# A graph network on one core: relational tables as two fp32r parts instead of three bf16 parts, and the loads at the start of the second relational layer issued earlier

## The chip, the cores and the metric

The kernel runs on one core of a Trainium2 chip. The metric is the device time of one execution in microseconds (us), lower is better. The median of three runs before the change is 2020.77 us (2017.62 to 2021.79). The outputs must equal the reference's to float32 accuracy, up to a tolerance.

## The reference

A graph has 3125 nodes of 128 features and 100,000 edges (`src`, `dst`, sorted by `dst`), each with one of 8 types. Four graph networks run one after the other, each added to its input and normalised. The first three (three graph convolutions, one sum over neighbours, one isomorphism layer with two batch norms) are dense products with an adjacency matrix that the kernel builds. The change is in the fourth, a relational network of two layers:

```python
def rgcn_layer(x, src, dst, etype, W, W_root, b, num_rels):
    N = x.shape[0]
    do = W.shape[-1]
    h = jnp.einsum('ni,rio->rno', x, W)
    msg = h[etype, src]
    seg = dst * num_rels + etype
    sums = jax.ops.segment_sum(msg, seg, num_segments=N * num_rels)
    cnt = jax.ops.segment_sum(jnp.ones(msg.shape[0], x.dtype), seg, num_segments=N * num_rels)
    mean = sums / jnp.maximum(cnt, 1.0)[:, None]
    agg = mean.reshape(N, num_rels, do).sum(axis=1)
    return agg + x @ W_root + b
src, dst = (edge_index[0], edge_index[1])
h = rgcn_layer(x, src, dst, edge_type, W1, root1, b1, NUM_RELS)
h = jax.nn.relu(h)
return rgcn_layer(h, src, dst, edge_type, W2, root2, b2, NUM_RELS)
```

For every node and every edge type, the rows of the sources are averaged; the averages go through (layer one) or come out of (layer two) a matrix for each type.

## The kernel before

**Blocks and two ways of summing.** The nodes are 25 blocks of 128. For the first 15 blocks of destinations (`ND`, in the chunks `DENSE` of 4, 4, 4 and 3 blocks) the sum over edges of a type is a dense product: matrices of edge counts, bytes in DRAM (`rel`), are loaded by `load8` (L755) on SP's DMA queue, five source blocks at a time, cast to fp32r by `cast8` (L763) on ScalarE or VectorE, and multiplied by the table of source rows in `relation` (L873, matmul at L885). The table stands in SBUF as two fp32r parts, a rounded value and its rest (`split2`, L786; tile `hilo`), so each of 25 source blocks takes two matmuls of 512 (or 384) columns. For the last 10 blocks (`NG`) edges are **gathered**, 128 at a time, in tiles: `gathered` (L893) runs over 10 groups of up to 34 tiles, 321 in a layer. For a tile an indirect DMA on GpSimd's queue (L919) fetches 128 rows of the table from DRAM into `gx`; VectorE makes a one-hot matrix `oh` for four tiles at a time (L909) of 24 destinations x 8 types = 192 columns; TensorE multiplies each part of the rows by it (L927) into two PSUM banks of 512 columns. A tile whose 192 columns cross column 512 is split into two matmuls a part.

**Tables in DRAM.** For the gathering, x3 (the input of layer one) is stored in `xt_d`, and x after the first layer's matrices, one row for each type and node, in `ht_d`. Both hold a row as three bf16 parts that add up to the float32 value. `store3` (L792) makes them: ScalarE rounds, VectorE subtracts, ScalarE rounds the rest, VectorE subtracts again, and SP's queue stores the 768 bytes a row.

**Order.** The order is written out by hand: `gathered` is a generator, and after every five source blocks of a dense product (ten matmuls) `fill` (L866) runs it some steps on, about 1.9 in layer one and 2.1 in layer two; a step is a tile. In layer one, each finished chunk goes through `linear1` (L950), which multiplies by the matrices of both layers and stores `ht_d` with `store3` (L978); gathered chunks do so too, from `put1`. After the last dense chunk the rest of the gathering runs alone (L1014).

**Between the layers.** In layer two `fetch(r)` (L1018) brings `ht_d`'s rows for type r back in five pieces: a load on SP's queue into `back`, two additions on VectorE that rebuild float32 (L1027, L1028), and `split2` into a `hilo` pair (L789 on ScalarE, L790 on VectorE). `fetch(0)` is called at L1068, when layer one has ended; `fetch(r + 1)` after the first chunk of type r. The final products with `root2` (L1036) go ahead of the first dense product. In layer two all five casts of a chunk are ScalarE's (L1073); in layer one, VectorE takes three of five.

**Making x3.** In a loop over seven chunks (L849), TensorE transposes, `normalise` runs on VectorE and ScalarE, `split2` fills the pair `xs`, and `stored` (L846) calls `store3` for `xt_d`. Tiles of a pool have a fixed number of buffers (`bufs`); a tile's writer waits until the readers of the buffer's earlier content are done. `hilo` and `hT` share two buffers with the tag "big".

## Time and profile before

The profiled execution took 2027.4 us, its span from the first to the last instruction is 2025.5 us; the three timed runs lie between 2017.62 and 2021.79. Mean granted TensorE clock 0.975.

| engine | busy us | share of span | instructions |
|---|---|---|---|
| TensorE (PE) matmul | 1794.3 | 89% | 11523 |
| TensorE weight load (PEld) | 1387.0 | 68% | 11523 |
| VectorE (DVE) | 1205.1 | 59% | 2055 |
| ScalarE (ACT) | 1253.0 | 62% | 1118 |
| GpSimd (POOL) | 859.5 | 42% | 717 |

Stages, by the first and last start of their lines: lists and matrices until 408 us; the dense networks (L628) 408 to 835; x3 from 835; layer one's dense products from 861, its gathers 895 to 1485, its end near 1511; layer two from 1511 to the end.

The costliest groups of the relational part (engine, line, operation, shape, count, busy us, mean ns of one):

| group | count | busy us | mean ns |
|---|---|---|---|
| PE L885 fp32r matmul, 512 columns | 2400 | 622.2 | 405 |
| PE L885 fp32r matmul, 384 columns | 800 | 170.1 | 357 |
| PEld L885 weight load 128x128 f32 | 3200 | 576.5 | 190 |
| PE L927 bf16 matmul, 192 columns | 1644 | 194.1 | 250 |
| PE L927 bf16 matmul, 160 / 32 columns | 114 / 114 | 16.3 / 14.2 | 233 / 178 |
| PE L927 bf16 matmul, 128 / 64 columns | 114 / 114 | 15.5 / 14.3 | 221 / 193 |
| PE L927 bf16 matmul, 96 columns | 108 | 8.0 | 206 |
| PEld L927 weight load 128x128 bf16 | 2208 | 157.0 | 97 |
| ACT L767 cast to fp32r, 2560 / 1920 | 169 / 56 | 388.3 / 99.3 | 2329 / 1794 |
| DVE L767 cast to fp32r, 2560 / 1920 | 71 / 24 | 125.4 / 33.0 | 1769 / 1376 |
| POOL L919 gather from xt_d | 321 | 366.1 | 1140 |
| POOL L919 gather from ht_d | 321 | 326.2 | 1016 |
| DVE L909 one-hot, 768 bf16 | 152 | 83.9 | 553 |
| DVE L1027, L1028, L790 (640 each) | 40 each | 32.6, 32.4, 32.1 | 824, 824, 822 |
| ACT L789 (640) | 40 | 27.8 | 723 |
| store3 of ht_d: ACT L798, L800; DVE L799, L801 | 50 to 54 each | 29.2, 33.4; 34.3, 37.2 | 583, 619; 686, 689 |

Matmuls are pipelined, and the mean of one contains its latency; the cost of one in a row of them is the distance from start to start. "PE" is the multiplication, "PEld" the load of its stationary operand, which overlaps it. A releaser is what ended an idle time; "issue" means that the profile shows nothing that the engine waited for.

### The profile page before, as it was taken

To read this page: it belongs to the slowest core of one execution; us is meant where nothing else is said; L and a number is where in the kernel's file an instruction comes from. 1 tells how busy PE (TensorE), PEld (TensorE's weight loads), DVE (VectorE), ACT (ScalarE), POOL (GpSimd) and SP (SyncE) were. 2 spreads that over 40 slices of the span, in tenths; PEclk is the share of its full clock that TensorE was granted. 3 is DMA by queue.
4 is the path that set the end of the run, shared out by engine and by line. 5 is a ranking of instruction groups with operands and counts; after the bars stand their busy time and mean duration, and the time that the engine had idled before them with its cause. 6 is when DMAs were issued, how large, how long until landed. Compare 5 with 4: busy or idle time off the path is not lost.

```text
span 2025.5 us, 30183 instructions
## 1 busy us (share of the span) xinstructions
PE 1794.3 (89%) x11523; PEld 1387.0 (68%) x11523; DVE 1205.1 (59%) x2055; ACT 1253.0 (62%) x1118; POOL 859.5 (42%) x717
## 2 busy tenths in 40 slices
PE   2677676669999999889999999999999999999897
PEld 1555555458888888667577567758757777777676
DVE  6999998777768863475455345435346444434424
ACT  3999997757888666663233333233338777777774
POOL 5315624120000000027777267706716666666664
PEclk9999998889999999999999999999999999999998
DMA  4766776667888887477677457737659887888773
GB/s 100 277 271 266 291 287 237 247 189 232 255 259 257 251 268 235 140 225 190 177 212 207 148 171 209 188 101 198 184 151 269 243 228 220 235 240 245 196 204 101
DMA packets 398932, 435.67 MB, mean 215 GB/s; under 512 B 27166, under 2 KB 355838, under 8 KB 398776
## 3 DMA queue, kind: packets, MB, share of 16 engines
q1 hardware_dynamic: 346274, 336.92, 53.0%
q0 software_dynamic: 33632, 67.07, 12.9%
q10 hardware_dynamic: 18870, 29.66, 4.9%
q8 instruction: 92, 1.51, 0.3%
q14 instruction: 64, 0.52, 0.1%
HBM read 319.07 MB, written 114.46 MB: 214 GB/s over the span
## 4 chain that ended last, share of the span: by engine, by line
PE 57%; ACT 4%; issue 3%; DVE 3%; another core or an unknown queue 2%; DMA 1%; ACTq 0%; SPq 0%; DVEq 0%
PE acc L885 30%; PE acc L628 8%; PE x L927 8%; PE mi L962 4%; PE mi L975 4%; ACT m L767 3%; PE mi L966 1%; DMA back<-ht_d 1%; PE mi L650 0%; PE x L836 0%; PE mi L740 0%; DVE hilo L790 0%; ACT mf L611 0%; DVE f L1027 0%
## 5 line engine op out<-in xcount | busy, mean ns | idle before, releaser
L885 PE MATMUL acc<-m,hilo 128*128 128x512 f32 (+1 forms) x3200 | 792.3, 393 | 22.8 <-ACT m L767 10.8
L767 ACT CAST m<-m 128x2560 fp32r<-128x2560 uint8 (+1 forms) x225 | 486.8, 2196 | 372.5 <-PE acc L885 148.7
L885 PEld LDWEIGHTS acc<-m,hilo 128*128 128x128 f32 x3200 | 576.5, 190 | 130.3 <-issue 17.6
L919 POOL DMA_INDIRECT gx<-xt_d,gsrc x321 | 366.1, 1140 | 638.5 <-DVE z L1007 413.7
L919 POOL DMA_INDIRECT gx<-ht_d,gsrc x321 | 326.2, 1016 | 200.1 <-issue 72.0
L628 PE MATMUL acc<-mf,halves 128*128 128x512 f32 (+1 forms) x1750 | 383.9, 377 | 11.5 <-DVE mf L613 11.0
L628 PEld LDWEIGHTS acc<-mf,halves 128*128 128x128 f32 x1750 | 320.4, 190 | 60.4 <-DVE mf L613 11.9
L611 ACT CAST mf<-m 128x2560 fp32r<-128x2560 bf16 (+1 forms) x126 | 263.7, 2100 | 67.3 <-PE acc L628 34.8
L927 PE MATMUL x<-oh,gx 128*128 128x192 bf16 (+5 forms) x2208 | 227.1, 239 | 5.5 <-issue 5.2
L927 PEld LDWEIGHTS <-gx 128*128 128x128 bf16 x2208 | 157.0, 97 | 99.2 <-issue 89.6
L767 DVE CAST m<-m 128x2560 fp32r<-128x2560 uint8 (+1 forms) x95 | 158.5, 1670 | 110.6 <-issue 40.3
L909 DVE TENSOR_TENSOR oh<-iota,gkey 128x768 bf16<-128x768 bf16 (+1 forms) x170 | 90.3, 532 | 208.5 <-PE x L927 143.2
L342 ACT CAST rb<-bld 128x800 uint16<-128x800 f32 x240 | 180.0, 847 | 6.5 <-PE bld L339 6.5
L339 PE MATMUL bld<-rhq,rlo 128*128 128x200 bf16 x960 | 124.2, 253 | 49.4 <-ACT rb L342 36.5
L290 POOL DMA_INDIRECT ew<-pk,ptr x26 | 72.7, 2797 | 193.9 <-DVE ptr L285 189.6
L339 PEld LDWEIGHTS <-rlo 128*128 128x128 bf16 x960 | 86.9, 98 | 85.3 <-issue 80.9
L613 DVE CAST mf<-m 128x2560 fp32r<-128x2560 bf16 (+1 forms) x49 | 97.5, 1989 | 70.1 <-PE acc L628 69.9
L191 DVE TENSOR_TENSOR lo<-iota,kT 128x4096 bf16<-128x4096 bf16 x50 | 114.2, 2283 | 11.1 <-PE bld L356 11.1
L191 DVE TENSOR_TENSOR rhq<-iota,kT 128x6400 bf16<-128x6400 bf16 x30 | 104.4, 3480 | 0.0
L975 PE MATMUL mi<-wr,hT 128*128 128x512 f32 x200 | 93.4, 601 | 2.5 <-issue 1.6
L359 ACT CAST at<-bld 128x800 bf16<-128x800 f32 x100 | 79.4, 835 | 20.7 <-PE bld L356 20.6
L270 POOL DMA_INDIRECT g<-in_dst,irow x26 | 76.6, 2947 | 22.9 <-DVE crow L265 9.8
(238 smaller groups left out, 1624.4 us busy)
## 6 DMA issues: line engine op xcount, KB each, us to landing
m<-rel SPq DMA_DIRECT2D x240, 320.0 KB
rel<-rb SPq DMA_DIRECT2D x120, 400.0 KB
m<-adj SPq DMA_DIRECT2D x60, 640.0 KB
m<-adj_t SPq DMA_DIRECT2D x40, 640.0 KB
m<-adj SPq DMA_DIRECT2D x45, 480.0 KB
adj_t<-at SPq DMA_DIRECT2D x25, 800.0 KB
adj<-av SPq DMA_DIRECT2D x25, 800.0 KB
ht_d<-t SPq DMA_DIRECT2D x50, 384.0 KB
```

Of the source, the lines that this page charges most:

```text
L191: return nc.vector.tensor_tensor(o, (iota2 if of is None else of)[:, None, :width, :].to_broadcast([P, PU // 2, width, 2]), k[:, :, None, ...
L339: nc.tensor.matmul(pt[:, k, : R * NB], lo2[:, j // 2, :, j % 2], hq[:, j // 2, :, j % 2], start=True, stop=True)
L342: nc.scalar.copy(rb[:, :, j0 : j0 + 4], pt[:, :, : R * NB].rearrange("p j q -> p q j"))
L611: nc.scalar.copy(v, src)
L613: nc.vector.tensor_copy(v, src)
L628: nc.tensor.matmul(acc[:, :w], x[:, 5 * g + k, :], mf[:, k, :w], start=(g == 0 and k == 0 and i == 0), stop=(more is None and g == 4 and k ...
L767: casts_by[on_act] = nc.scalar.copy(v, src) if on_act else nc.vector.tensor_copy(v, src)
L885: nc.tensor.matmul(acc[:, :w], x[:, 5 * g + k, :], m[:, k, :w], start=(g == 0 and k == 0 and i == 0), stop=(g == 4 and k == 4 and i == 1),)
L909: ins = nc.vector.tensor_tensor(oh[:, : nt // 2], iota2[:, None, : GW * R, :].to_broadcast([P, nt // 2, GW * R, 2]), gkey[:, g, t : t + nt ...
L919: nc.gpsimd.indirect_dma_start(out=gx.rearrange("p i c -> p (i c)"), out_offset=None, in_=table[:], in_offset=bass.IndirectOffsetOnAxis(ap ...
L927: nc.tensor.matmul(acc[a // 512][:, a % 512 : a % 512 + z - a], gx[:, i, :], oh[:, t % 4 // 2, a - c0 : z - c0, t % 2], start=(a // 512 no ...
L975: nc.tensor.matmul(o, hT[:, a, cols(b, 1)], wr[:, a, r : r + 4, :].rearrange("p r c -> p (r c)"), start=(a == 0), stop=(a == 1))
```

## The change

- `xt_d` and `ht_d` hold float32 words, two fp32r parts a row: 1024 bytes instead of 768.
- `store3` becomes `store2`: a rounding on ScalarE and a subtraction on VectorE, with 3 buffers instead of 4. For `xt_d` nothing is computed any more: `stored` writes the two parts from `xs`, in two DMAs a chunk.
- In `gathered`, `oh` is fp32r (4 bytes an element, no pairs of tiles interleaved), `gx` holds two fp32r parts in 10 buffers instead of 12, and a tile takes two fp32r matmuls instead of three bf16 ones (four instead of six where it is split).
- `fetch` loads the two parts straight into the pair, two DMAs for each of five pieces; no arithmetic is left. Between the end of the last dense chunk of layer one and the rest of its gathering, the first five `load8` of layer two and the first three pieces of `fetch(0)` (the 15 dense blocks) are issued; the other two follow the gathering.
- In layer two VectorE takes two of every five casts.

```diff
--- before.py
+++ after.py
@@ -118,8 +118,8 @@
 
     inv_n = dram.tile([SB * 2 * P, R], F32, name="inv_n")
 
-    xt_d = dram.tile([NP, 3 * D], BF, name="xt_d")
-    ht_d = dram.tile([R * NP, 3 * D], BF, name="ht_d")
+    xt_d = dram.tile([NP, 2 * D], F32, name="xt_d")
+    ht_d = dram.tile([R * NP, 2 * D], F32, name="ht_d")
 
     xa = const.tile([P, NB, D], F32, name="xa")
     iota2 = const.tile([P, R * NB, 2], BF, name="iota2")
@@ -789,17 +789,14 @@
             nc.scalar.copy(hi, x)
             nc.vector.tensor_sub(lo, x, hi.bitcast(F32))
 
-        def store3(rows, x):
+        def store2(rows, x):
 
             n = x.shape[1]
-            t = rp.tile([P, 4, 3, D], BF, name="t3", bufs=4)
-            a, b, c = [t[:, :n, i, :] for i in range(3)]
-            e = rp.tile([P, 4, D], F32, name="e3", bufs=3)[:, :n, :]
-            nc.scalar.copy(a, x)
-            nc.vector.tensor_sub(e, x, a)
-            nc.scalar.copy(b, e)
-            nc.vector.tensor_sub(c, e, b)
-            nc.sync.dma_start(rows, t[:, :n].rearrange("p b i c -> p b (i c)"))
+            t = rp.tile([P, 4, 2, D], F32R, name="t2", bufs=3)
+            hi, lo = [t[:, :n, i, :] for i in range(2)]
+            nc.scalar.copy(hi, x)
+            nc.vector.tensor_sub(lo, x, hi.bitcast(F32))
+            nc.sync.dma_start(rows, t[:, :n].rearrange("p b i c -> p b (i c)").bitcast(F32))
 
 
         def batchnorm(bst, i):
@@ -844,7 +841,9 @@
         hT = rp.tile([P, 2, NP], F32, name="hT", tag="big", bufs=2)
 
         def stored(m0, nb):
-            store3(xt_d[m0 * P : (m0 + nb) * P].rearrange("(b p) c -> p b c", p=P), x3[:, m0 : m0 + nb, :])
+            rows = xt_d[m0 * P : (m0 + nb) * P].rearrange("(b p) (i c) -> i p b c", p=P, i=2)
+            for i, x in enumerate(xs):
+                nc.sync.dma_start(rows[i], x[:, m0 : m0 + nb, :].bitcast(F32))
 
         for c, (m0, nb) in enumerate(CH):
             t = bank(("acc", "x", "x", "x", "x", "mi", "mi")[c])
@@ -905,29 +904,28 @@
                 for t in range(GT[g]):
                     if t % 4 == 0:
                         nt = min(4, GM - t)
-                        oh = rp.tile([P, 2, GW * R, 2], BF, name="oh", bufs=3)
+                        oh = rp.tile([P, 4, GW * R], F32R, name="oh", bufs=3)
                         ins = nc.vector.tensor_tensor(
-                            oh[:, : nt // 2],
-                            iota2[:, None, : GW * R, :].to_broadcast([P, nt // 2, GW * R, 2]),
-                            gkey[:, g, t : t + nt].rearrange("p (j i) -> p j i", i=2)[:, :, None, :]
-                            .to_broadcast([P, nt // 2, GW * R, 2]),
+                            oh[:, :nt],
+                            iota2[:, None, : GW * R, 0].to_broadcast([P, nt, GW * R]),
+                            gkey[:, g, t : t + nt, None].to_broadcast([P, nt, GW * R]),
                             op=OP.is_equal,
                         )
                         if g == 0 and t < 12:
                             behind(ins, first_cast)
-                    gx = rp.tile([P, 3, D], BF, name="gx", bufs=12)
+                    gx = rp.tile([P, 2, D], F32R, name="gx", bufs=10)
                     nc.gpsimd.indirect_dma_start(
-                        out=gx.rearrange("p i c -> p (i c)"), out_offset=None, in_=table[:],
+                        out=gx.rearrange("p i c -> p (i c)").bitcast(F32), out_offset=None, in_=table[:],
                         in_offset=bass.IndirectOffsetOnAxis(ap=rows[:, g, t : t + 1], axis=0),
                     )
                     c0 = first(t) * R
                     ends = [c0] + ([512] if c0 < 512 < c0 + GW * R else []) + [c0 + GW * R]
-                    for i in range(3):
+                    for i in range(2):
                         for a, z in zip(ends, ends[1:]):
                             nc.tensor.matmul(
                                 acc[a // 512][:, a % 512 : a % 512 + z - a], gx[:, i, :],
-                                oh[:, t % 4 // 2, a - c0 : z - c0, t % 2],
-                                start=(a // 512 not in seen), stop=(t == GT[g] - 1 and i == 2),
+                                oh[:, t % 4, a - c0 : z - c0],
+                                start=(a // 512 not in seen), stop=(t == GT[g] - 1 and i == 1),
                                 skip_group_check=True,
                             )
                             seen.add(a // 512)
@@ -936,6 +934,15 @@
                           iv[:, n * R : min(wn, n + 64) * R]) for n in range(0, wn, 64)]
                 yield from put(b, wn, parts) or ()
                 yield
+
+        def fetch(r, lo=0, hi=NB, pieces=None):
+
+            pieces = pieces or pair()
+            rows = ht_d[r * NP : (r + 1) * NP].rearrange("(b p) (i c) -> i p b c", p=P, i=2)
+            for m0 in range(lo, hi, 5):
+                for i, x in enumerate(pieces):
+                    nc.sync.dma_start(x[:, m0 : m0 + 5, :].bitcast(F32), rows[i][:, m0 : m0 + 5])
+            return pieces
 
         with tc.tile_pool(name="f_z", bufs=1, reuse_waits="tile") as zp:
             w1 = zp.tile([P, R, O1], F32, name="w1")
@@ -975,7 +982,7 @@
                             nc.tensor.matmul(o, hT[:, a, cols(b, 1)],
                                              wr[:, a, r : r + 4, :].rearrange("p r c -> p (r c)"),
                                              start=(a == 0), stop=(a == 1))
-                        store3(ht_d.rearrange("(r n) c -> n r c", r=R)[b * P : (b + 1) * P, r : r + 4],
+                        store2(ht_d.rearrange("(r n) c -> n r c", r=R)[b * P : (b + 1) * P, r : r + 4],
                                blocks(o))
                         yield
 
@@ -1011,24 +1018,14 @@
                 for _ in linear1(z, m0, nb):
                     fill(work, 0.95 * 2.0)
                 turn[0] = None
+
+            early.extend([load8(0, *DENSE[0], g), None] for g in range(5))
+            hr = fetch(0, 0, ND)
             for _ in work:
                 pass
+            fetch(0, ND, NB, hr)
 
         with tc.tile_pool(name="f_hr", bufs=1, reuse_waits="tile") as hp:
-            def fetch(r):
-
-                pieces = pair()
-                for m0 in range(0, NB, 5):
-                    t = hp.tile([P, 5, 3, D], BF, name="back", bufs=2)
-                    r0 = r * NP + m0 * P
-                    nc.sync.dma_start(t.rearrange("p b i c -> p b (i c)"),
-                                      ht_d[r0 : r0 + 5 * P].rearrange("(b p) c -> p b c", p=P))
-                    f = hp.tile([P, 5, D], F32, name="f", bufs=2)
-                    nc.vector.tensor_add(f, t[:, :, 0], t[:, :, 1])
-                    nc.vector.tensor_add(f, f, t[:, :, 2])
-                    split2(pieces, m0, 5, f)
-                return pieces
-
             oT = hp.tile([P, NP], F32, name="oT")
             for m0, nb in CH:
                 o = psum.tile([P, 512], F32, name="mi", tag="mi", bufs=2)
@@ -1065,12 +1062,11 @@
 
             work = gathered(ht_d, gsrc[1], put2)
             ahead[0] = -14
-            hr = fetch(0)
             for r in range(R):
                 nxt = None
                 for i, (m0, nb) in enumerate(DENSE):
                     inv = load_inv(r, m0, nb)
-                    acc = relation(r, m0, nb, hr, work, 2.1, (1, 1, 1, 1, 1))
+                    acc = relation(r, m0, nb, hr, work, 2.1, (1, 0, 1, 0, 1))
                     s = hp.tile([P, 512], F32, name="s", bufs=2)
                     w = nb * P
                     nc.vector.tensor_mul(s[:, :w], acc, inv)
```

## The prediction, made before the change was run

> **What bounds the kernel now.** I read the chain of waits first, then the windows by stage, then the timeline of the two relational layers, where all of the edits lie.
>
> ```profile
> PE 57%; ACT 4%; issue 3%; DVE 3%; another core or an unknown queue 2%; DMA 1%; ACTq 0%; SPq 0%; DVEq 0%
> PE acc L885 30%; PE acc L628 8%; PE x L927 8%; PE mi L962 4%; PE mi L975 4%; ACT m L767 3%; PE mi L966 1%; DMA back<-ht_d 1%; PE mi L650 0%; PE x L836 0%; PE mi L740 0%; DVE hilo L790 0%; ACT mf L611 0%; DVE f L1027 0%
> ```
>
> TensorE sets the end; the dense relational product (L885) and the gathered product (L927) are its largest shares. The windows' columns are the stretch, its length, then PE, PEld, DVE, ACT and POOL busy, clock, DMA share, GB/s.
>
> ```profile
> 860.00:870.00 10.00, 6.93 (x32) 5.34 (x31) 9.55 (x42) 6.75 (x17) 0.00 (x0) 0.90 0.68 207
> 1200.00:1300.00 100.00, 100.00 (x575) 77.64 (x574) 53.32 (x50) 32.66 (x14) 76.08 (x65) 1.00 0.75 204
> 1522.00:1540.00 18.00, 15.61 (x67) 11.51 (x67) 14.37 (x19) 14.32 (x13) 14.15 (x13) 1.00 0.92 265
> 1600.00:1700.00 100.00, 95.07 (x575) 76.02 (x574) 35.84 (x57) 74.38 (x39) 66.56 (x68) 1.00 0.84 237
> ```
>
> Four regimes: VectorE-bound while x3 is made (860 to 880), TensorE-bound in layer one, a stall of everything at the start of layer two, then TensorE-bound again with ScalarE at 74% and DMA at 0.84. So what counts is PE time per gathered tile.
>
> ```profile
> 943.97 2.58 PE L885 MATMUL acc<-m,hilo 128*128 128x512 f32 x10
> 946.39 0.43 PE L927 MATMUL x<-oh,gx 128*128 128x192 bf16 x3
> 946.60 2.58 PE L885 MATMUL acc<-m,hilo 128*128 128x512 f32 x10
> 949.02 0.69 PE L927 MATMUL x<-oh,gx 128*128 128x192 bf16 x6
> 949.49 2.59 PE L885 MATMUL acc<-m,hilo 128*128 128x512 f32 x10
> ...
> 1970.34 2.58 PE L885 MATMUL acc<-m,hilo 128*128 128x512 f32 x10
> 1972.76 0.70 PE L927 MATMUL x<-oh,gx 128*128 128x128 bf16 x12
> 1973.28 2.57 PE L885 MATMUL acc<-m,hilo 128*128 128x512 f32 x10
> ```
>
> Durations contain latency, so I take start to start. Ten dense matmuls and one tile: 946.60-943.97 = 2.63. With two tiles: 949.49-946.60 = 2.89. A whole tile (three bf16 matmuls of 192) therefore costs 0.26 us. Ten dense matmuls alone take 10 x 0.22, so 2.63-2.20-0.26 leaves 0.17 for the **switch** from dense to gathered; the weight loads before L927 idle 343 times on "issue", so 343 switches. Two tiles that cross column 512 (12 matmuls) take 2.94-2.20-0.17 = 0.57, 0.29 each. The groups by shape give 1644/3 = 548 whole tiles and 38+38+18 = 94 split ones. Gathering costs PE now 548 x 0.26 + 94 x 0.29 + 343 x 0.17 = 142+27+58 = **227 us** over both layers.
>
> **The change, part by part.**
>
> *Gathered matmuls, the large term.* Two instead of three a tile, fp32r instead of bf16: 548x2 + 94x4 = 1472. No row shows fp32r under 384 columns. The nearest:
>
> ```profile
> 1440.58 1.71 PEld L885 LDWEIGHTS acc<-m,hilo 128*128 128x128 f32 x10
> ...
> 811.83 1.05 PE L735 MATMUL acc<-eps_i,xa 128*128 128x128 f32 x8
> ...
> 1487.62 3.62 PE L962 MATMUL mi<-zg,w 128*128 128x256 f32 x16
> 1505.32 1.95 PE L962 MATMUL mi<-zg,w 128*128 128x64 f32 x16
> ```
>
> The first is ten fp32r matmuls of 384: (1.71-0.19)/9 = 0.169 apart. Fp32r of 512 is 0.22 apart, so fp32r streams at some 0.4 ns a column, and 192 would stream in 0.08. Plain f32 is issued as two instructions a matmul, each at half that rate: 256 columns (3.62-0.38)/15 = 0.216 apart, 128 columns (1.05-0.27)/7 = 0.111, but 64 columns still (1.95-0.28)/15 = 0.112. That 0.11 is a floor which the 4-byte weight load sets, since 64 columns stream faster; bf16 loads have none so high (tiles of split matmuls are 0.05 apart). **Value taken: 0.112 us each**, 1472 x 0.112 = 165, because fp32r is one instruction with the same 128x128 f32 load. The switch goes to 0: dense fp32r to f32 (L628 to L650) shows none; at most it stays, +58. So -62: 31 a layer. Low bound: 0.08 each, 118, so -109. High bound: fp32r that short costs what f32 does: 192 columns interpolate to 0.165 an instruction, two instructions 0.33, so 548 x 0.66 = 362, and split tiles 0.9 to 1.0, 88: 450, **+223**. Break-even is at (227+13)/1472 = 0.163 us a matmul, 13 being the two small gains below.
>
> *One-hot* (L909): 768 elements to 4 bytes; f32 rows of 512 and 640 take 0.69 and 0.82, so 0.96 against 0.55, +66 us of VectorE in all. VectorE is 36 to 55% busy there and three tiles ahead; at 0. Uncovered, it would cost those 66.
>
> *xt_d from xs*: removes 14 VectorE operations (4 x 1.37 + 3 x 1.09 = 8.7 us) and 14 ScalarE ones (7.9) in the stretch where VectorE is 95% busy. Dense work runs unbroken only from 887. Of 8.7 I take **-6** (bounds 0 and -8.7). SP issues 14 stores instead of 7, 0.36 each, beside it.
>
> *store2*: one ScalarE and one VectorE operation less for each of 50 ht_d stores (0.62, 0.69). The PSUM bank is freed by the operations that stay, so 0.
>
> *The start of layer two.* Its fetch waited for the last ht_d store:
>
> ```profile
> 1512.43 6.63 DMA back<-ht_d
> ...
> 1521.40 3.88 DMA back<-ht_d
> ```
>
> The first 100 dense matmuls ran from 1521.4 to 1554.3, 33 us, for 22 us of dense work and some 3.5 of gathering: 7 us lost. The five loads and six fetch transfers move on SP's queue ahead of the tail's 4-block stores; ht_d rows below block 15 are stored by then. Queued behind them are the last ht_d stores, for which POOL's layer-two gathers wait. 11 issues x 0.36 = 4 us, covered by the 36 us tail; the fetch's wait for stored rows covers at worst 6.6 more, exposed. **-7** (bounds -11, +7).
>
> *Layer two.* VectorE loses 40 x 3 x 0.82 = 98 us of rebuilding and gets 48 x 1.77 + 16 x 1.38 = 107 us of casts plus 33 of one-hots; ScalarE loses 48 x 2.33 + 16 x 1.79 + 28 = 168. Neither bounds after. But transfers grow: gathered rows 768 to 1024 bytes (+10.5 MB), fetched rows the same (+6.5 MB, in twice the number of transfers). From 1512 to 2026 queue q0 takes 22.8% of 514 us for 31.6 MB, 3.7 us a MB, and q1 45.6% for 66.7 MB, 3.5. So +39 and +23 on 400 us of DMA time: 462 in a layer of under 500, a share of 0.94, where the steadiest stretch (500 to 700) shows 0.87. And POOL:
>
> ```profile
> L919 POOL DMA_INDIRECT gx<-xt_d,gsrc x72 | 84.7, 1176 | 27.1 <-issue 15.5 <-PE x L927 8.1 <-remote 1.9
> ...
> L919 POOL DMA_INDIRECT gx<-ht_d,gsrc x68 | 67.7, 996 | 33.7 <-issue 16.5 <-PE x L927 8.2 <-remote 5.6
> ```
>
> These are 110 us of layer one, with 35 us of VectorE casts, and 100 us of layer two, with none. A gather is 0.18 longer beside casts, 13 us for 35, or 0.37 us per us of cast. For 107 us of casts, +40: 321 x (1.0+0.3) + 40 = 457, under the layer's 500, so covered, with little to spare. Of the two PE gains here (31 and 7) I keep **-15** for those two near-limits. If DMA can't pass 0.87, the layer lasts 462/0.87 = 531: +17.
>
> One rule speaks against these casts. The Trainium skill, page "SBUF — State Buffer", section "Who interferes with whom", says that VectorE's casts in a two-port mode hold the pair that GpSimd needs and block it fully. By it all 107 us would be added to POOL: 417+107 = 524, and layer two would be some 20 longer rather than 15 shorter, total about 2006. The row above shows about a third of that, and the measurement decides.
>
> *Layer one* takes its 31 less 1 for larger stores: **-30** (POOL, 1.44 a tile, has 139 us of waiting on PE there; uncovered, the 30 is lost).
>
> **Sum**: -6 -30 -15 = -51. The profiled execution took 2027.4 (span 2025.5, 2 around it), so 1976; it stands 0.33% above the median, 2020.8, on which the sum gives **1970**.
>
> **The rivals.**
> *A, the forecast, 50%*: 1970; its own range 1938 (all of -109's half, -8.7, -11) to 2000.
> *B, slower, 27%*: fp32r under 256 columns runs no faster than f32. Place: L927. Price 0.33 against 0.112 a matmul, deciding from 0.163 on: 2020.8+223-13 = 2231, less 10 to 20 of layer two's 33 us of PE idling that a slower PE hides: about 2215. For it: nobody runs fp32r short here, all fp32r products are 384 or 512 wide. Against: L885 shows one instruction and pure streaming at 384.
> *C, 12%*: the fp32r load is not hidden behind so short a matmul: 0.11+0.08 = 0.19 each, 280, +53-13: about 2060; with 0.169, the shortest fp32r spacing seen, 249: 2030. Against: f32 of 64 columns hides it.
> *D, 11%*: the PE gain doesn't arrive, because layer two is held by DMA at 0.87 (-6-30+17: 2002) or the early fetch sits behind the stores on SP anyway (-6-30-8: 1977 to 2010).
>
> **From the cases**: faster is A and most of D, 0.59; slower is B and most of C, 0.37; the same, 0.04. A difference under 0.2% (4 us) can't be told from none. The range must take in C and the lower third of B: 1938 to 2210.
>
> **What would show it.** L927 fp32r starts 0.11 apart (A), 0.17 to 0.19 (C) or 0.33 (B); a dense group with two tiles at 2.65 rather than 2.89; L909 at 0.96; no idle before L927's loads; dense work unbroken from 881 instead of 887; layer two's first product without gaps; POOL's gathers near 1.13 and DMA above 0.9 there. The prediction is wrong if short fp32r isn't load-bound, or if layer two turns DMA- or POOL-bound.

## The result, and the profile after

The changed kernel takes 2026.46 us (median of 13, 2017.52 to 2033.16); the kernel before, beside it, 2020.77 (median of 13). The ratio is **1.0047**, with a 95% interval of 1.0030 to 1.0064: slower by half a per cent, where 2.5% faster was forecast. The profiled execution took 2024.0 us (span 2022.2); against the span of 2025.5 before it stands the other way round than the medians, so single executions can't carry a difference of this size.

In these executions, and in those of e1 to e4, engines also stand idle where the profile names nothing that they wait for (in layer two of before, from 1522 to 1960, ScalarE's casts 58 us on "issue" or an unknown queue) and the kernel before takes 2021 to 2031 us, while beside all the other experiments it takes 1967 without such waits; why is not known, and every ratio below is to the kernel before as it ran beside that experiment.

The chain of waits after:

```profile
PE 56%; issue 4%; DVE 3%; DMA 2%; ACT 1%; POOL 1%; another core or an unknown queue 0%; DVEq 0%; ACTq 0%; POOLq 0%
```

TensorE still sets the end (57% before), but DMA has 2% of it instead of 1, and GpSimd, which had none, 1%. Windows after (stretch, length, busy PE, PEld, DVE, ACT, POOL, clock, DMA share, GB/s):

```profile
860.00:870.00 10.00, 7.17 (x28) 4.69 (x27) 8.43 (x36) 6.91 (x15) 0.00 (x0) 1.00 1.05 320
1200.00:1300.00 100.00, 100.00 (x505) 82.75 (x504) 59.35 (x50) 32.34 (x15) 80.16 (x66) 1.00 0.78 226
1522.00:1540.00 18.00, 18.00 (x83) 14.72 (x82) 6.66 (x6) 10.58 (x5) 6.15 (x6) 1.00 1.13 311
1600.00:1700.00 100.00, 93.56 (x490) 81.46 (x489) 51.09 (x54) 43.23 (x20) 73.92 (x69) 0.97 0.89 256
```

The gap at the start of layer two is closed (18.00 of 18), VectorE has air at 860, and ScalarE's load in layer two is down from 74 to 43. But TensorE, which had 95.07 of 100 us at 1600, now has 93.56, at a lower clock, with DMA up to 0.89. The timeline of TensorE in layer one, after:

```profile
942.03 2.52 PE L884 MATMUL acc<-m,hilo 128*128 128x512 f32 x10
944.38 0.59 PE L925 MATMUL x<-oh,gx 128*128 128x192 f32 x4
944.81 2.51 PE L884 MATMUL acc<-m,hilo 128*128 128x512 f32 x10
```

Ten dense matmuls and two tiles: 944.81-942.03 = 2.78 (before 2.89). Four fp32r matmuls of 192 columns take 944.81-944.38 = 0.43, so 0.108 each: forecast A's price. The gain per group is small and then it vanishes: layer one's end, after, and below it before (the number in brackets is TensorE's idle time and what ended it):

```profile
1485.90 0.47 PE L925 MATMUL x<-oh,gx 128*128 128x192 f32 x2 [1.80 <-DMA gx<-xt_d,gsrc]
1487.96 0.43 PE L925 MATMUL x<-oh,gx 128*128 128x192 f32 x2 [1.59 <-DMA gx<-xt_d,gsrc]
1488.89 1.04 PE L925 MATMUL x<-oh,gx 128*128 128x160 f32 x4 [0.50 <-DMA gx<-xt_d,gsrc]
1490.80 1.06 PE L925 MATMUL x<-oh,gx 128*128 128x128 f32 x4 [0.87 <-DMA gx<-xt_d,gsrc]
...
1493.23 3.51 PE L969 MATMUL mi<-zg,w 128*128 128x64 f32 x16
```

```profile
1498.58 2.87 PE L927 MATMUL x<-oh,gx 128*128 128x192 bf16 x37
1503.27 2.00 PE L962 MATMUL mi<-zg,w 128*128 128x64 f32 x16 [1.68 <-DVE zg L991]
```

Before, the last gathered tiles stood ready and ran in one go; after, TensorE reaches them sooner, waits four times for rows, and then runs at half speed (3.51 us for 16 products that took 2.00; the granted clock of 1490 to 1500 is 0.50). The last product of layer one's last dense chunk (`mi<-z,w` in `linear1`) came 15.6 us earlier (1450.0 against 1465.6), the first dense product of layer two only 4.5 (1516.9 against 1521.4), and layer two then took 505.3 instead of 504.1.

The same pair in runs b0 and a0 (the two kernels unaltered) is clearer: medians of 1967.25 and 1997.93, ratio **1.0148** [1.0126, 1.0169]. Their windows in layer two, before and after:

```profile
1600.00:1700.00 100.00, 100.00 (x619) 81.46 (x618) 46.54 (x72) 84.50 (x47) 76.02 (x74) 1.00 0.90 257
1700.00:1800.00 100.00, 100.00 (x621) 81.79 (x620) 48.84 (x85) 84.71 (x48) 75.26 (x74) 1.00 0.91 257
```

```profile
1600.00:1700.00 100.00, 95.55 (x512) 83.69 (x511) 52.42 (x54) 44.26 (x21) 76.62 (x68) 0.97 0.94 267
1700.00:1800.00 100.00, 94.57 (x494) 80.95 (x493) 54.20 (x67) 44.55 (x22) 79.58 (x68) 0.98 0.97 274
```

Before, TensorE has no gap at all there; after, it has 5% and a lower clock. The gathers of layer two, before and after (count, busy us, mean ns, then idle time before them and what ended it):

```profile
L919 POOL DMA_INDIRECT gx<-ht_d,gsrc x321 | 327.2, 1019 | 151.9 <-issue 61.9 <-PE x L927 48.8 <-DMA ht_d<-t 34.5
```

```profile
L917 POOL DMA_INDIRECT gx<-ht_d,gsrc x321 | 365.0, 1137 | 140.8 <-issue 57.9 <-PE x L925 41.4 <-DMA hilo<-ht_d 25.0
```

GpSimd is 37.8 us longer at them (365.0-327.2), and TensorE's waits in the changed kernel's layer two begin with rows and casts (us in total, times, longest):

```profile
PE x L925 <- DMA gx<-ht_d,gsrc: 15.3, 17, 2.1
PE acc L884 <- DVE m L767: 8.1, 2, 4.5
```

Layer two (its first dense product to the end of the span) takes 457.2 us before and 491.2 after. By stages the 38.3 us between the two profiled spans (1962.9 and 2001.2; the medians differ by 30.7) are: x3 -5.8 (first `z` at 885.0 and 879.2), layer one from there to its end +10.4, `root2` -0.3, first chunk of layer two -3.7 (15.2 and 11.5 after the `root2` products), the rest of layer two +37.7. In the first pair the same stages give -10.5, +6.3, -0.3, -4.0 and +5.2. These are single executions, and a0's is the slowest of its four; the four profiles with the changed kernel's casts and all its fetches at once (a0, e5, e6, e7) have layer two between 483 and 491 us, so a few us there mean nothing by themselves.

### The profile page after: what moved, and what is told of

The parts are those of the page before. It is cut to its first block, busy times and chain, and to the rows that moved or that the text cites. A ratio compares the mean times of both kernels' runs of the same rounds, so it can differ in the third digit from the quotient of the medians.

```text
span 2022.2 us, 28533 instructions
## 1 busy us (share of the span) xinstructions
PE 1783.6 (88%) x10787; PEld 1438.0 (71%) x10787; DVE 1245.0 (62%) x1935; ACT 1061.0 (52%) x950; POOL 895.5 (44%) x717
## 3 DMA queue, kind: packets, MB, share of 16 engines
q0 software_dynamic: 33632, 88.10, 15.2%
## 4 chain that ended last, share of the span: by engine, by line
PE 56%; issue 4%; DVE 3%; DMA 2%; ACT 1%; POOL 1%; another core or an unknown queue 0%; DVEq 0%; ACTq 0%; POOLq 0%
PE acc L884 30%; PE acc L628 7%; PE x L925 7%; PE mi L982 4%; PE mi L969 4%; DMA gx<-ht_d,gsrc 2%; DVE m L767 1%; POOL gx L917 1%; PE mi L973 1%; PE mi L1033 1%; DMA gx<-xt_d,gsrc 0%; PE mi L650 0%; PE x L833 0%; PE mi L740 0%
## 5 line engine op out<-in xcount | busy, mean ns | idle before, releaser
L884 PE MATMUL acc<-m,hilo 128*128 128x512 f32 (+1 forms) x3200 | 775.0, 389 | 15.2 <-issue 6.0
L767 ACT CAST m<-m 128x2560 fp32r<-128x2560 uint8 (+1 forms) x161 | 353.0, 2199 | 528.1 <-PE acc L884 190.7
L917 POOL DMA_INDIRECT gx<-ht_d,gsrc x321 | 357.4, 1113 | 162.7 <-issue 74.7
L767 DVE CAST m<-m 128x2560 fp32r<-128x2560 uint8 (+1 forms) x159 | 266.2, 1675 | 233.6 <-issue 103.7
L925 PEld LDWEIGHTS x<-oh,gx 128*128 128x128 f32 x1472 | 217.0, 193 | 62.3 <-issue 19.0
L925 PE MATMUL x<-oh,gx 128*128 128x192 f32 (+5 forms) x1472 | 230.4, 281 | 22.7 <-DMA gx<-ht_d,gsrc 12.8
L908 DVE TENSOR_TENSOR oh<-iota,gkey 128x768 fp32r<-128x768 bf16 (+1 forms) x170 | 154.2, 910 | 99.7 <-PE x L925 65.1
L290 POOL DMA_INDIRECT ew<-pk,ptr x26 | 79.8, 3071 | 191.2 <-DVE ptr L285 187.0
L798 DVE TENSOR_TENSOR t<-mi,t 128x512 fp32r<-128x512 f32 x50 | 34.5, 691 | 110.7 <-ACT t L797 91.6
```

What stands on the lines that cost most here:

```text
L767: casts_by[on_act] = nc.scalar.copy(v, src) if on_act else nc.vector.tensor_copy(v, src)
L884: nc.tensor.matmul(acc[:, :w], x[:, 5 * g + k, :], m[:, k, :w], start=(g == 0 and k == 0 and i == 0), stop=(g == 4 and k == 4 and i == 1),)
L908: ins = nc.vector.tensor_tensor(oh[:, :nt], iota2[:, None, : GW * R, 0].to_broadcast([P, nt, GW * R]), gkey[:, g, t : t + nt, None].to_bro ...
L917: nc.gpsimd.indirect_dma_start(out=gx.rearrange("p i c -> p (i c)").bitcast(F32), out_offset=None, in_=table[:], in_offset=bass.IndirectOf ...
L925: nc.tensor.matmul(acc[a // 512][:, a % 512 : a % 512 + z - a], gx[:, i, :], oh[:, t % 4, a - c0 : z - c0], start=(a // 512 not in seen), ...
```

## The experiments

All 18 runs. "Ratio" is to the kernel before as it ran beside the run; "layer one" is the start of the `root2` products and "layer two" the time from its first dense product to the end, both of the profiled execution; "one fetch" leaves out seven of the eight fetches, so that all types use the first type's rows; "finish" is the kernel's function for the last additions and the normalisation; "gather" is the mean of a POOL gather from `ht_d`; the last column is TensorE's longest sum of waits in layer two.

| run | edit of the changed kernel | ratio, 95% | layer one ends | layer two | gather, ns | TensorE waits for |
|---|---|---|---|---|---|---|
| e1 | casts of layer two on ScalarE | 1.0021 [1.0002, 1.0041] | 1512.3 | 510.9 | 1027 | ScalarE's casts 16.9 |
| e2 | fetch in pieces | 1.0022 [1.0003, 1.0040] | 1512.3 | 510.6 | 1124 | gathered rows 13.4 |
| e3 | one fetch | 1.0002 [0.9984, 1.0021] | 1512.0 | 507.2 | 1129 | ScalarE's casts 8.2 |
| e4 | 14 gather and 2 store buffers | 1.0025 [1.0007, 1.0044] | 1510.7 | 510.1 | 1127 | "issue" 19.5 |
| b0 | (the kernel before) | | 1495.1 | 457.2 | 1019 | VectorE (finish) 2.5 |
| a0 | none | 1.0148 [1.0126, 1.0169] | 1499.7 | 491.2 | 1137 | gathered rows 15.3 |
| e5 | early part undone | 1.0155 [1.0136, 1.0175] | 1502.8 | 487.1 | 1128 | gathered rows 13.2 |
| e6 | four tiles at a time | 1.0195 [1.0176, 1.0214] | 1504.6 | 489.1 | 1134 | gathered rows 24.4 |
| e7 | layer one's gathers denser | 1.0075 [1.0058, 1.0091] | 1487.1 | 483.0 | 1132 | gathered rows 14.2 |
| e8 | one fetch, casts on ScalarE | 0.9980 [0.9969, 0.9991] | 1501.1 | 452.5 | 1010 | VectorE (finish) 4.1 |
| f1 | one fetch | 1.0152 [1.0137, 1.0167] | 1501.0 | 480.8 | 1132 | gathered rows 17.3 |
| c2 | casts on ScalarE, denser | 1.0130 [1.0108, 1.0152] | 1485.7 | 499.9 | 1008 | ScalarE's casts 29.5 |
| c3 | as c5, 14 gather and 2 store buffers | 1.0046 [1.0030, 1.0061] | 1492.4 | 465.9 | 1016 | ScalarE's casts 12.0 |
| c5 | as c2, fetch in pieces | 1.0008 [0.9998, 1.0019] | 1483.4 | 475.3 | 1012 | ScalarE's casts 14.4 |
| c6 | as c5, 10 load buffers | 0.9988 [0.9980, 0.9997] | 1483.5 | 467.2 | 1008 | ScalarE's casts 10.2 |
| c7 | as c6, casts as changed | 1.0066 [1.0049, 1.0082] | 1484.5 | 482.4 | 1137 | gathered rows 14.3 |
| h1 | new tables in layer one alone | 0.9990 [0.9981, 0.9999] | 1489.7 | 461.3 | 1023 | gathered rows 3.2 |
| h2 | the kernel before, denser | 0.9995 [0.9986, 1.0004] | 1495.0 | 457.3 | 1021 | VectorE (finish) 2.5 |

### One suspect at a time: e1 to e4

```diff
@@ e1 @@
-                    acc = relation(r, m0, nb, hr, work, 2.1, (1, 0, 1, 0, 1))
+                    acc = relation(r, m0, nb, hr, work, 2.1, (1, 1, 1, 1, 1))
@@ e2 @@
-                        nxt = fetch(r + 1)
...
+                        step = 5 * (i - 1) + g
+                        if r + 1 < R and step >= 0 and step % 3 == 0:
+                            fetch(r + 1, 5 * (step // 3), 5 * (step // 3) + 5, nxt)
...
@@ e3, f1 @@
-                        nxt = fetch(r + 1)
+                        nxt = hr
@@ e4 @@
-            t = rp.tile([P, 4, 2, D], F32R, name="t2", bufs=3)
+            t = rp.tile([P, 4, 2, D], F32R, name="t2", bufs=2)
-                    gx = rp.tile([P, 2, D], F32R, name="gx", bufs=10)
+                    gx = rp.tile([P, 2, D], F32R, name="gx", bufs=14)
```

> The changed kernel, with all casts of layer two on ScalarE again. Changed kernel: gathers of layer two mean 1.11 us (before 1.02), TensorE waits 12.8 us there for gathered rows and 4 for VectorE casts; median 2026.5 against 2020.8 before. Theory V (VectorE's casts slow GpSimd and come late themselves): gathers back to 1.02 to 1.04, the waits for gathered rows under 4 us, time 2005 to 2013, ratio about 0.995. Theory F (the five pieces of a fetch, ten transfers issued at once, crowd out the gathered rows): the gathers shorten, the waits for rows stay at 10 to 15, time 2020 to 2027. Theory B (10 gather buffers instead of 12 let every late row through to TensorE): as F.

> The changed kernel, but each fetch of layer two (types 2 to 8) goes out piece by piece, one piece of two transfers after every third group of the second, third and fourth chunk, instead of all ten transfers at once after the first chunk. Same bytes, same transfers. Theory F (burst): the stretches of 10 us with DMA above 1.0 go, TensorE's waits for gathered rows in layer two fall from 12.8 to under 4 us and the low clock that follows each stall with them; 12 to 18 us faster than the changed kernel, 2008 to 2014, ratio about 0.996. Theories V and B: within 5 us of the changed kernel, 2021 to 2030.

> The changed kernel with one fetch alone: the rows of the first type serve all eight types of layer two, so seven fetches (23 MB) are left out and the dense sums of types 2 to 8 are made of the first type's rows. Theory F, and any theory in which DMA holds layer two: DMA share of 1600 to 1900 falls from 0.94 to about 0.75, waits for gathered rows under 3 us, layer two shorter by 15 to 25 us, 2001 to 2011. Theory V or B: DMA falls as much, but the time stays within 6 us of 2026. Against the paced fetch it tells volume (only this one gains) from bursts (both gain alike).

> The changed kernel with 14 gather buffers instead of 10 (room made by 2 store buffers instead of 3). Theory B: the tail of layer one, where TensorE waits 1.80, 1.59, 0.87 us at a time for gathered rows and then runs at half clock, loses these waits, 8 to 10 us; layer two's 12.8 us of waits for rows fall below 5; in all 12 to 20 us, 2006 to 2014, ratio 0.993 to 0.997. Theories F and V: the tail gains at most 4, layer two less than 4, time 2020 to 2027.

The changed kernel itself didn't run beside these four. Against its 1.0047 [1.0030, 1.0064] of the first pair their ratios are lower, but only e3's interval lies clear of it, and none shortens layer two (507 to 511 us, 505 in the first pair). What each did was to move the wait. With ScalarE's casts the gathers are short again (1027 ns) and the waits for rows halve to 6.3 us, but the casts come late (16.9). With 14 buffers the rows are never late (1.0 us), but the dense products are, by 19.5 without a named cause. No theory came out whole: V and B have the waits for rows right, but not the time, and F's pieces (e2) leave these waits at 13.4.

### The early part, the switch, the tail: e5 to e7

```diff
@@ e5 @@
-            early.extend([load8(0, *DENSE[0], g), None] for g in range(5))
-            hr = fetch(0, 0, ND)
-            fetch(0, ND, NB, hr)
...
+            hr = fetch(0)
@@ e6 @@
-            while ahead[0] >= 1.0:
-                next(work, None)
-                ahead[0] -= 1.0
+            while ahead[0] >= 4.0:
+                for _ in range(4):
+                    next(work, None)
+                ahead[0] -= 4.0
@@ e7 @@
-            ahead[0] = -34
+            ahead[0] = -30
-                    acc = relation(r, m0, nb, xs, work, 0.95 * (1.0 + nb / 4), (0, 1, 0, 1, 0))
+                    acc = relation(r, m0, nb, xs, work, 0.97 * (1.0 + nb / 4), (0, 1, 0, 1, 0))
-                    fill(work, 0.95 * 2.0)
+                    fill(work, 0.97 * 2.0)
```

> The changed kernel without the early part: the five loads and the first fetch of layer two go out where they did before the change, after layer one has ended. Theory E (the early transfers get in the way of layer one's tail: SP holds ht_d stores behind fetches that wait, and the crowded DMA delays the last gathered rows): the tail from the last dense z to the first dense product of layer two, 78 us in the changed kernel against 67 before, shrinks to 66 to 70, while the first dense product of layer two is late again by some 7 to 9 us; in all the time is equal to the changed kernel within 4 us. Theory P (GpSimd's pace sets the tail, 321 gathers of 1.155+0.30 us): the tail stays at 75 to 78, and the time grows by 6 to 10 us, ratio 1.008 to 1.010.

> The changed kernel with gathered tiles taken four at a time after every second group of ten dense products instead of about two after each. Same matmuls. It measures the switch from dense to gathered products: with 0.11 us a switch, left over from 343 switches, two groups and four tiles should take 4.40+0.92+0.11 = 5.43 instead of 5.54. If TensorE bounds layer one, that is some 8 us less there; in layer two nothing if GpSimd's gathers hold it (theory P), 8 more if TensorE does. Time 2014 to 2020 for both layers, 2018 to 2022 for layer one alone; 2026 or more if four tiles at once drain the ring of 10 gather buffers.

> The changed kernel with layer one's gathers spread a little denser: 0.97 steps instead of 0.95, beginning four steps earlier, so that no tile is left when the dense chunks end (in the changed kernel the last 12 or so run alone: TensorE waits 4.8 us for their rows and then runs 20 us at 0.5 to 0.9 of the clock). Theory T (the gain of layer one is lost in this tail): waits for xt_d rows go, and the products of the last 64 columns take 1.95 again instead of 3.51; 6 to 12 us less, 2014 to 2020, ratio 0.997 to 1.001. Theory P in its strong form (GpSimd's gathers bound the whole of layer one): the waits only move into the dense part, and the time stays within 4 us of 2026.

**e5**: from the last `z` to layer two's first dense product it is 80.2 us, against 81.9 in a0 and 66.2 in b0: the early transfers aren't what spoils the tail, so theory E falls. But they bring nothing either, and the 6 to 10 us that theory P gave them aren't there: the first chunk of layer two ends 11.5 us after the `root2` products with them and without, and the ratio is the same. What is left to bring the 3.7 us is the fetch that needs no arithmetic; no run takes it apart from the casts, which changed there too.

**e6**, TensorE's timeline:

```profile
1185.04 4.83 PE L885 MATMUL acc<-m,hilo 128*128 128x512 f32 x20
1189.70 1.03 PE L926 MATMUL x<-oh,gx 128*128 128x192 f32 x8
1190.57 4.84 PE L885 MATMUL acc<-m,hilo 128*128 128x512 f32 x20
```

Two groups and four tiles take 1190.57-1185.04 = 5.53, not 5.43, and in the changed kernel twice 2.77: halving the switches saves nothing, so none are left to save. The four tiles at once drain the ring of rows (24.4 us of waits).

**e7** ends layer one 12.6 us before a0 and its 64-column products take 1.96 again: theory T holds, with 12 to 15 us instead of 6 to 12 (beside it, e5 and e6 end layer one 16 and 18 us later). h2 gives the same order to the kernel before and moves nothing (1495.0): the tail was lost through the change.

### Two limits at once: e8, f1, c2

e8 has the edits of e1 and e3, c2 those of e1 and e7.

> Layer two with both suspected loads taken away at once: one fetch (the rows of the first type serve all eight types, seven fetches are left out and the dense sums of types 2 to 8 are made of the wrong rows) and all casts on ScalarE. Alone, the one brought 0.45% and the other 0.26%. Theory N (near-limits that hide each other: with one relieved, the other holds layer two at 505 to 511 us): together they give more than the sum, layer two 485 to 495 us, 2001 to 2010, ratio 0.990 to 0.995. Theory A (the two add): ratio near 0.9975. If TensorE's own order (casts late on ScalarE, 2.33 us each on three buffers) holds it: no better than the fetch alone, 1.000.

> As the earlier run with one fetch (seven fetches of layer two left out, the first type's rows used for all eight), casts as in the changed kernel, on a chip where the kernel before takes about 1967 us. There layer two (first dense product to the end) took 457 us before, 491 in the changed kernel, and 452 with one fetch and all casts on ScalarE. Theory P (GpSimd's gathers, 1.13+0.30 us by 321 = 459, hold it by themselves): 474 to 482 us, PE still waits for gathered rows with DMA far below 1. Theory F (DMA holds it, casts on VectorE cost little): 452 to 462.

> The changed kernel, unaltered, so that its ratio and its trace stand beside those of its variants on one chip. Where an earlier chip gave 2020 to 2031 us for the kernel before, another gave 1968, and the time of the changed kernel there isn't known. Theory P (GpSimd's gathers hold layer two: 321 of 1.13 us and 0.30 between them, 459 us, where TensorE needs about 440): on a chip like the second, ratio 1.010 to 1.018, and GpSimd's gathers and the 0.30 after each fill over 95% of the time from layer two's first gather to its last. On a chip like the first, ratio 1.003 to 1.006 and 90 to 93%. If GpSimd isn't the bound: 1.003 to 1.006 on either.

> The kernel before, unaltered, with its trace on the same chip. Theory P: from layer two's first gather to its last, gathers (1.01 to 1.02 us, and 0.30 each) fill at most 92%; TensorE is busy over 97% of layer two on a chip where the whole takes 1968 us.

> The changed kernel with two lines altered: all casts of layer two on ScalarE, and layer one's gathers a little denser (0.97 steps, beginning four steps earlier). Theory P with the tail of layer one: layer one ends 13 to 17 us earlier, the gathers of layer two fall to 1.02 us, layer two is 10 to 20 us shorter: ratio to the kernel before 0.985 to 0.998, that is 25 us or more below the changed kernel. If ScalarE's casts hold layer two instead (2.33 us each, four of them late by 1 to 6 us on the first chip): the gain is the tail's alone, 10 to 15 us below the changed kernel.

With a0 these make a table of two by two for layer two:

| | casts 2 of 5 on VectorE | all on ScalarE |
|---|---|---|
| eight fetches | 491.2 (a0) | 499.9 (c2) |
| one fetch | 480.8 (f1) | 452.5 (e8) |

Taking away seven fetches alone gains 10 (by the medians nothing: 1.0152 and 1.0148), moving the casts to ScalarE alone loses 9, both together gain 39: theory N. c2 has e7's edit as well; against e7's 483.0 it loses 17. The 10 are hardly more than the spread named above, the 39 are far beyond it. As a ratio e8's 0.9980 lies where theory A had it (0.9975), but A started from a changed kernel 0.5% slow; on the 1.5% here it would have asked for a gain from each edit alone, and there is none. c2 missed what was expected of it either way: its median is 3.4 us below a0's. In f1 GpSimd is what is left: its 321 gathers with 0.30 between them fill 363.3+96.3 = 459.6 of the 471.6 us from first to last, 97%, and TensorE waits 17.3 us for rows at a DMA share of 0.77 to 0.79. f1's window:

```profile
1700.00:1800.00 100.00, 94.04 (x497) 81.41 (x495) 54.47 (x68) 44.26 (x22) 78.97 (x70) 0.98 0.78 224
```

TensorE has gaps although DMA is far from full, and neither VectorE nor ScalarE is. In a0 they fill (365.0+96.3)/480.9 = 96%, as expected. The 92% expected of b0 was wrong, however: there it is (327.2+96.3)/444.7 = 95%. **GpSimd was already nearly level with TensorE before the change.** In c2 GpSimd is relieved, and the loads from `rel` become late instead; two views of c2, a line of TensorE's timeline and the windows:

```profile
1576.54 4.64 PE L884 MATMUL acc<-m,hilo 128*128 128x512 f32 x10 [5.08 <-ACT m L767]
```

```profile
1560.00:1570.00 10.00, 8.63 (x44) 7.11 (x43) 2.34 (x3) 4.56 (x2) 6.66 (x8) 1.00 1.10 327
1570.00:1580.00 10.00, 4.92 (x17) 3.89 (x16) 0.96 (x1) 5.84 (x3) 3.43 (x3) 0.73 1.05 304
```

TensorE waits 5 us for a ScalarE cast while ScalarE itself is idle for 42% of that stretch: its bytes aren't there (its own waits for loads from `rel` sum to 32.5 us in layer two). DMA stands above 1.0, as in two or three stretches of 10 us after the start of each of these fetches of ten transfers. After the stall the ten products take 4.64 instead of 2.51.

### Easing the transfers: c3, c5, c6, c7

c5 has the edits of e1, e2 and e7; c3 and c6 add to it:

```diff
@@ c3 @@
-            t = rp.tile([P, 4, 2, D], F32R, name="t2", bufs=3)
+            t = rp.tile([P, 4, 2, D], F32R, name="t2", bufs=2)
-                    gx = rp.tile([P, 2, D], F32R, name="gx", bufs=10)
+                    gx = rp.tile([P, 2, D], F32R, name="gx", bufs=14)
@@ c6 @@
-            m8 = rp.tile([P, 4, 5, P], U8, name="m8", bufs=6)
+            pool, tag, n = deep[0]
+            m8 = pool.tile([P, 4, 5, P], U8, name=tag, bufs=n)
...
+            deep[0] = (hp, "m8d", 10)
```

> As the kernel with two lines altered, and also each fetch piece by piece over the following chunks, and 14 gather buffers with 2 store buffers. Theory F (bursts of DMA make casts and rows late once GpSimd has room): 5 to 12 us below the kernel with two lines altered, ratio 0.98 to 0.993. If bursts don't count: within 3 us of it.

> Three alterations of the changed kernel: all casts of layer two on ScalarE, layer one's gathers denser, fetches piece by piece. Against the run with the first two alone (layer two 500 us, 29.5 us of waits for ScalarE's casts, which wait for loads from rel) it shows what bursts cost: theory F: layer two 466 to 475, ratio 1.000 to 1.004; if bursts don't matter: 495 to 500, ratio 1.013. Against the run that also has 14 gather buffers and 2 store buffers (layer one ended 6.7 us later there): the same layer two, and some 6 us less.

> The three alterations, and 10 buffers of their own for the loads from rel in layer two (6 in the changed kernel), so that loads can run ahead over a fetch. Theory L (once GpSimd and bursts are eased, layer two waits only for late loads): the 12 us of waits for ScalarE's casts go, with the low clock after them; layer two 442 to 455, ratio 0.985 to 0.995. If DMA's volume itself holds it (124 MB at 300 GB/s are 413 us, at 270 GB/s 459): 460 or more, ratio about 1.0.

> The same with the changed kernel's casts, two of five on VectorE: late loads and bursts are eased alike, so the difference to the run before is the casts alone. Theory P: gathers 1.13 instead of 1.02 us, 321 by 0.11 = 35 us more for GpSimd, which then fills 95% or more of layer two's gathers: layer two 472 to 482, 25 to 30 us more than with ScalarE. If GpSimd has room: the same time within 5 us.

The fetch in pieces takes layer two from 499.9 to 475.3 (c5): bursts matter, once GpSimd has room. Deeper loads bring 8 more (c6), not the 20 hoped for; 467 is what was expected if DMA's volume holds the layer, but that isn't shown: from 1600 to 1800 DMA runs at 1.03 to 1.05 and TensorE is busy for 99.6% all the same, and 9.7 of the 10.2 us of waits for ScalarE's casts end in two short stretches, 1563 to 1573 and 1844 to 1853. c3's two store buffers cost it 9 us in layer one (ScalarE waits 45.6 us for finished stores there, 3.5 in c5). Its layer two, expected to equal c5's, is 9 us shorter, but in the fastest of its ten executions; by the medians c3 is 6 us slower than c5 as a whole. The gathers of c6 and of c7, which differ in the casts alone (count, busy us, mean ns, idle before and its releasers):

```profile
L922 POOL DMA_INDIRECT gx<-ht_d,gsrc x321 | 323.6, 1008 | 180.7 <-PE x L930 61.1 <-issue 60.9 <-DMA hilo<-ht_d 47.6
```

```profile
L922 POOL DMA_INDIRECT gx<-ht_d,gsrc x321 | 365.0, 1137 | 154.4 <-issue 59.1 <-DMA hilo<-ht_d 47.7 <-PE x L930 30.0
```

41 us more of GpSimd, and layer two is 15.2 us longer (15.4 by the medians of the whole): half of the 25 to 30 expected. That c6's own waits for late loads hide the other half is likely, not shown.

### What is left: h1, h2

h2 is the kernel before with the edits of e7. h1 starts from e1 and e7 and takes layer two back to three bf16 parts (table, gathers and fetch), with 9 gather buffers and 3 and 2 for the stores:

```diff
@@ h1 @@
-    ht_d = dram.tile([R * NP, 2 * D], F32, name="ht_d")
+    ht_d = dram.tile([R * NP, 3 * D], BF, name="ht_d")
...
-                        store2(ht_d.rearrange("(r n) c -> n r c", r=R)[b * P : (b + 1) * P, r : r + 4],
+                        store3(ht_d.rearrange("(r n) c -> n r c", r=R)[b * P : (b + 1) * P, r : r + 4],
...
-            hr = fetch(0, 0, ND)
-            fetch(0, ND, NB, hr)
```

> The change in layer one alone: xt_d and layer one's gathers as two fp32r parts, layer two (ht_d, its gathers, fetches and casts) as in the kernel before, except that its first five loads are issued early; layer one's gathers denser (0.97 steps, four steps earlier); 9 gather buffers, and 3 and 2 buffers for the ht_d stores. Theory (layer two is where the change loses, by GpSimd and DMA; layer one gains once its tail is gone): layer one ends 9 to 13 us before that of the kernel before, layer two takes 455 to 460 us as before: 1950 to 1960 where the kernel before takes 1967, ratio 0.992 to 0.997. If three instead of four store buffers hold the tail: 0.997 to 1.000.

> The kernel before with layer one's gathers spread denser in the same way (0.97 steps, four steps earlier) and nothing else. It tells whether the tail was lost through the change or was there before. If the tail is the change's (before, the last gathered tiles stood ready in 12 buffers and ran 13 in a row without a wait): within 0.2% of the kernel before, 0.998 to 1.002. If the denser order gains by itself: 5 to 10 us, 0.995 to 0.998, and that much of the gain of the variants with it isn't the tables'.

With the tail mended, the new tables end layer one 11.6 us earlier than the old ones (c5 1483.4, h2 1495.0), of which 7.7 lie before the first `z`; in h1 it is 5.3, and why isn't shown (ScalarE waits only 0.2 us for its fewer store buffers). At the end of h1 little of it remains (0.9990, where 0.992 to 0.997 was expected): its layer two is 4.0 us longer than h2's, with its last tiles waiting for rows (3.2 us in all) where those of before ran through. c6 and h1 come out 0.1% below the kernel before. Their intervals end just under 1, but this is within the 0.2% that I called no change: no complete version here beats it for certain.

## Why the prediction was wrong

**The baseline of the gathered matmuls was mis-sized; this is the largest term.** The new price was right: 0.112 forecast, 0.108 measured, 548 x 0.21 + 94 x 0.43 = 155 us against 165. The old price, 227 us, was not, because "ten dense matmuls alone take 10 x 0.22" was wrong. A row of before, from the dense networks, had it:

```profile
503.89 11.62 PE L628 MATMUL acc<-mf,halves 128*128 128x512 f32 x49
515.34 0.83 PE L650 MATMUL mi<-w_L_gnn_W,pt 128*128 128x128 f32 x6
```

(515.34-503.89)/49 = 0.234. Ten take 2.34, and the rows of before in the prediction give the rest from start to start: dense 943.97 to 946.39 is 2.42, so the switch costs 0.08, not 0.17; two tiles take 0.47, one 0.21, a split one 0.26. That is 548 x 0.235 + 94 x 0.26 + 343 x 0.08 = 180. After, the switch is 0.01 (2.35 for ten), so 155+3 = 158. **-22 instead of -62**: 47 of the 227 us were dense time that I had booked to the tiles and the switch. That the switch goes was right; it was worth 24 us, not 58. Split tiles even lose (0.43 against 0.26), as their four fp32r matmuls take 0.11 each on average, with 160 and 32 columns as with 96 and 96. The -22, 11 a layer, is itself worked out from a few rows, and the traces show less: layer one's dense part gains 5.6 us, and layer two after its first chunk takes 441.0 in e8, which neither VectorE's casts nor the fetches hold, against 442.0 in b0 (before `finish` TensorE waits 7.5 us for VectorE's additions there, 2.5 in b0).

**Layer one, -30 forecast, +10.4 measured (b0, a0; +6.3 in the first pair).** The dense part gained 5.6 us (11.4 at the last `z`, less the 5.8 of x3); the tail from there to the `root2` products grew from 55.6 to 71.6. I had named the point, "uncovered, the 30 is lost", and dismissed it with 139 us in which GpSimd waits for TensorE. These lie earlier (from 1300 to 1400 GpSimd of the changed kernel is busy for 32 us, from 1200 for 80); at the end it is some tiles late, and a tile that waits costs clock as well: in a0 TensorE waits 6.6 us for rows there, and its granted clock is 0.50 from 1478.4 to 1498.8. More buffers alone don't mend it: e4's 14 took away all waits for `xt_d` rows, but layer one ended within 2 us of e1 to e3, its two store buffers costing what they won; an earlier start of the gathers (e7) does.

**Layer two, -15 forecast, +37.7 after its first chunk (+5.2 in the first pair).** GpSimd's part was right in size: +40 forecast, 365.0-327.2 = +37.8 measured. The step that failed is "under the layer's 500, so covered". Those 500 contained waits of the profiled execution; b0 needs 457 there, and e8, with the new tables and neither limit, 452. With VectorE's casts and one fetch it is 481 (f1), with all fetches and ScalarE's casts 500 (c2). Cover has to be measured against what the bound engine will need, not against the stretch as it ran. DMA was right in share (0.94 to 0.99), but I took 0.94 for a rate that suffices; it comes in bursts, and what is late is a load of 320 KB or a row that someone waits for. Of rival D the place was right; its 531 us for the layer weren't reached (505 in that execution).

**The Trainium skill**, page "SBUF — State Buffer", section "Who interferes with whom", warned of VectorE's casts. I had read its block as 107 us more for GpSimd, the length of all casts; but the page gives the ports to whichever of the two issues first, so that isn't what it asks for. c7 against c6 shows 41, 0.39 us for each us of cast, as layer one of before had (0.37). The size was the row's, the direction the page's. How the 41 come about can be read in a0, gathers on GpSimd and casts on VectorE:

```profile
1627.62 1.96 POOL L917 DMA_INDIRECT gx<-ht_d,gsrc  x1 [0.30 <-issue]
1633.97 0.94 POOL L917 DMA_INDIRECT gx<-ht_d,gsrc  x1 [0.30 <-DMA gx<-ht_d,gsrc]
```

```profile
1627.55 1.75 DVE L767 CAST m<-m 128x2560 fp32r<-128x2560 uint8 x1
1634.51 1.98 DVE L767 CAST m<-m 128x2560 fp32r<-128x2560 uint8 x1 [4.16 <-PE acc L884]
```

The first gather starts in a cast and ends 0.28 us after it (1629.58 and 1629.30); the second has run for 0.54 us when a cast starts, and takes its 0.94 as if alone. Of the 42 gathers of layer two that start with more than 0.7 us of a cast still to come, 32 end 0.27 to 0.29 us after the cast and 8 end 0.41 to 0.42 after it; none of the 16 whose only cast starts 0.52 to 0.91 us after them takes more than 0.95. So a gather that meets a cast early is held until about the end of the cast, not slowed by a share, and one that meets it late loses nothing: that is how 107 us of casts add 41.

**Right**: x3 -6 (-5.8); the one-hots at 0.95 us, and hidden (no wait of TensorE for one in a0). `store2` at nothing was not tested apart from the rest. **The start of layer two**, -7: -3.7, and not by the early issue (e5). The "33 us" for the first 100 dense matmuls run to 1554.3, where VectorE multiplies the sums of the second chunk; TensorE's hundredth starts near 1549.8, so some 4 us were lost, not 7. Rivals B and C fell with the 0.108 us spacing.

## What to carry to other kernels

Price an instruction from an unbroken run of its own kind; a difference of two estimates (2.63-2.20-0.26) collects all errors, and here it gave a cost that could be "saved". When two engines and the DMA are within 5% of each other, taking work off one gains nothing unless the others have room, and undoing one suspect at a time shows nothing: test them in pairs. Slack that an average shows (waits of the gathering engine, a layer's length) must lie where the change needs it.

## What the runs showed of the hardware

- An fp32r matmul of 192 columns with a 128x128 load starts every 0.108 us, one of 512 every 0.234.
- After a stall TensorE can be granted less: in the changed kernel 1.00 until 1488.3 and 0.50 for 17 us from there, after waits of 1.80 and 1.59 us; in a0 0.50 from 1478.4, after a single one of 1.77; and 0.73 in c2's stretch above, with one of 5.08, where ten products then take 4.64 instead of 2.51 us. So a stall can cost more than its length. Not every one does: c6 keeps 1.00 from 1556 to 1572, with a wait of 1.95 us in it. The Trainium skill, page "TensorE: Matmul & The Clock Gate", section "Part 1: The HAM clock gate", names an idle window of about 3.4 us for this; a0 shows that a shorter wait can do it too.
- An indirect gather of 128 rows takes GpSimd 0.94 us at best, whether a row has 768 or 1024 bytes, with 0.30 to the next. Beside VectorE's casts single ones take up to 1.98 (a0), without them up to 1.58 (b0), once 2.48 (e1); a gather that starts well inside a cast mostly ends 0.28 us after it.
- What remains open: why c6's loads still come late twice, and why the new tables gain TensorE less than its rows promise.
